# The first element of a two-stage graph kernel: another order of its loads, biases as rows, and the residual added on VectorE

## The chip, the cores and the metric

The kernel runs on one NeuronCore of a Trainium2 chip. It has five engines with an instruction stream each: TensorE (PE, matmuls; PEld in a profile is its weight load), VectorE (DVE), ScalarE (ACT), GpSimd (POOL) and SyncE (SP). SP issues most of the DMA transfers; GpSimd and ScalarE can issue some too. The metric is device time of one execution, in microseconds (us); lower is better. The kernel before took 2397.51 us, the median of three runs from 2396.07 to 2399.57 us.

## The reference, cut to what matters

Sixteen independent elements b, each with node features x (1024 x 128) and a dense matrix adj (1024 x 1024), all float32. Two stages, each with a residual and a layer norm without scale:

```
# stage 0
degree = adj.sum(-1)
nb     = einsum('id,ij->jd', x, adj) / degree
x1     = layernorm(x + relu(concat(x, nb) @ W.T + b))
# stage 1: four layers; layer l sees x1 or earlier layers' outputs
src = f @ ws + bs ;  dst = f @ wd + bd ;  own = f @ wn + bn
src_agg = (adj / row_norm) @ src          # rows scaled to length 1
dst_agg = (adj / column_norm).T @ dst     # columns scaled to length 1
f_next  = tanh(concat(src_agg, own, dst_agg) @ wu + bu)
# result
out = layernorm(x1 + f_4)
```

Stage 0 needs adj and x of the element, W (128 x 256) and b. Stage 1 needs for every layer the products of its weights with wu ("folded" weights), made once in the first element, and row and column norms of adj.

## The kernel before, in words

The order of work on every engine is written out by hand (manual_schedule, line 1041). Elements are run one after another; while element b is in its four layers, the loads, row sums, squares and stage 0 of element b + 1 are placed between its matmuls through "hooks". The first element has nothing ahead of it to hide in, so its stage 0 and the weight folding stand in a prologue of their own, lines 1047 to 1239, and parts of them in the hooks of its first layer (lines 1251 to 1306). The change touches only these.

**The loads of the prologue.** adj of element 0 is 4 MB. It is cut in two halves h of 512 rows, each half in two "row pairs" (PAIRS, in the order h = 1 and then h = 0), and every pair in G = 4 groups g of 32 partitions: a pair is four transfers of 256 KB (load_pair, lines 1054 to 1057). x is cut in the same way into eight transfers of 64 KB (load_nodes). Groups 0 and 1 (partitions 0 to 63) go on SP's queue, groups 2 and 3 (partitions 64 to 127) on GpSimd's. SP's order is: w0n (W, 128 KB), two groups of x for each half, two groups of each of the four pairs, b0c (the bias b), and then for each layer its weights and biases (fetch_weights, line 180), between them adj once more in another layout (load_rows, four times 1 MB). A bias is 128 values that go to one value on each partition, so one transfer of 128 pieces of 4 bytes; there are 17 of them. SP issues through eight completion semaphores in turn: a transfer is issued only when the one eight places ahead of it has landed.

**Its matmuls.** PE first transposes W (w0tr, lines 1102 to 1105), then for each half transposes x (to_xT), starts the residual's bank with x times the identity (with_x, line 1165) and starts pw, W's first half times x (weights_of_x, line 1157). Then the "gathers" (line 1131), 16 matmuls of 128 x 512 that sum x over the rows of adj, four for each row pair. ScalarE squares the rows of each pair, VectorE sums them (squares_of). The inverse degrees are spread over partitions by transposes (degree_row, factor_bank at line 354); scaled, weights_of_agT and with_y (line 1171, which adds the transposed result to the residual's bank) end stage 0 of a half; norm_stats and norm_write or norm_write_act make x1n, to_x1 its transpose.

**The weights.** fold_begin (line 199) and fold_end (line 222) make a layer's folded weights: transposes and small products on PE, copies by ScalarE, both through the two banks of small(). Layers 0 and 1 are folded in the prologue, 2 and 3 in hooks 5, 8, 9 and 12 of the first layer (lines 1302 to 1304). messages (line 686) makes the layer's messages in four groups; plain_layer (line 827) is the first element's first layer, whose products are d (destination, on a) and z (source, on at). row_factors0 (line 1252) gathers the inverse row norms, rinv, with which scale_rows scales the second copy of adj on ScalarE; transpose_rows turns it into at on VectorE.

## Time and profile before

One execution was profiled: 2396.57 us, of which 2394.8 us are the span from the first to the last instruction; 1.77 us lie around it.

| | before |
|---|---|
| median of three runs | 2397.51 us |
| the profiled execution, and its span | 2396.57 us, 2394.8 us |
| busy: PE, DVE, ACT, POOL | 2377.7, 2089.2, 980.3, 273.8 us |
| PE's first gather begins at | 13.31 us |
| PE busy from 13.3 to 20.0, 20 to 30, 30 to 40 us | 6.69, 9.97, 9.67 us |
| PE busy from 40 to 50, 50 to 60, 60 to 70 us | 8.40, 9.76, 9.80 us |
| PE and DVE busy from 100 to 120 us | 17.79, 18.14 us |

Times in the views are counted from the start of the span. A row of a timeline gives the start, the duration, the engine, the line of code, the operation with what it writes and reads, and how many instructions were joined; in brackets stands the idle time before it and what ended it. A matmul of float32 appears as two records. "SPq" rows are SP issuing a transfer, not the transfer itself.

### The profile page before, as it was taken

What the parts mean: (1) busy time and instruction counts of PE and PEld (TensorE: products, weight loads), DVE (VectorE), ACT (ScalarE), POOL (GpSimd) and SP (SyncE); (2) the same over time, 40 slices, a digit from 0 to 9 for tenths busy, and PEclk for the clock granted to TensorE, in tenths of its full rate; (3) what the DMA queues carried; (4) which work ended last, traced back from release to release, by engine and by line L of the source; (5) the groups of instructions that cost most, each with busy time, mean ns of one, the idle gap of its engine ahead of it and who ended that gap; (6) DMA issues with size and microseconds to landing.
All of it is one profiled execution on the core that took longest, in us unless ns stands there. A gap on an engine that the chain in (4) does not pass through costs nothing.

```text
span 2394.8 us, 39324 instructions
## 1 busy us (share of the span) xinstructions
PE 2377.7 (99%) x15293; PEld 1288.4 (54%) x15293; DVE 2089.2 (87%) x2814; ACT 980.3 (41%) x1842; POOL 273.8 (11%) x102
## 2 busy tenths in 40 slices
PE   8999999999999999999999999999999999999998
PEld 4444554645556455554655546455464555645555
DVE  5998888999889989889988889888899888998954
ACT  5524345253343524435244452534525344352322
POOL 4101111001111011110111110111100111101110
PEclk9999999999999999999999999999999999999999
DMA  9527244262633627335272442634426253362400
GB/s 206 123 75 146 69 114 90 70 148 57 137 75 81 138 48 157 61 97 116 55 163 56 107 97 71 147 69 111 91 69 151 57 132 78 80 141 48 100 22 22
DMA packets 365897, 232.03 MB, mean 97 GB/s; under 512 B 152784, under 2 KB 336848, under 8 KB 365712
## 3 DMA queue, kind: packets, MB, share of 16 engines
q1 hardware_dynamic: 364944, 227.16, 42.6%
q0 software_dynamic: 768, 2.36, 0.4%
q8 instruction: 121, 1.98, 0.4%
q14 instruction: 64, 0.52, 0.1%
HBM read 209.59 MB, written 19.84 MB: 96 GB/s over the span
## 4 chain that ended last, share of the span: by engine, by line
PE 95%; DVE 2%; DMA 1%; SPq 1%; issue 1%; ACT 0%; POOLq 0%; DVEq 0%
PE m L1005 40%; PE z L1005 29%; PE pt L247 9%; PE pt_z L247 5%; PE m_f L583 5%; PE z_f L583 2%; PE pw L247 2%; PE m3s L1005 1%; PE z L851 1%; DMA wm<-in_L_gnn_ws_dram 1%; PE pt_p L247 1%; SPq L640 1%; DVE acc L331 0%; DMA a<-in_adj_dram 0%; PE d L851 0%
## 5 line engine op out<-in xcount | busy, mean ns | idle before, releaser
L1005 PE MATMUL m<-a,t 128*64 128x512 f32 x1008 | 434.6, 593 | 0.2 <-DVE t L711 0.2
L1005 PE MATMUL m<-at,t 128*64 128x512 f32 x1008 | 418.5, 592 | 0.0
L1005 PE MATMUL m<-Q,S 128*64 128x512 f32 x880 | 394.0, 593 | 0.0
L1005 PE MATMUL m<-T,S 128*64 128x512 f32 (+1 forms) x1040 | 393.5, 573 | 0.0
L456 POOL TENSOR_TENSOR rs<-ve,mhalf 128x32 f32<-128x32 f32 x30 | 191.9, 6396 | 987.9 <-DVE ve L454 987.9
L1005 PE MATMUL z<-at,t 128*64 128x512 f32 x504 | 229.2, 592 | 0.0
L1005 PE MATMUL z<-at,S 128*64 128x512 f32 x504 | 228.3, 593 | 0.0
L1005 PE MATMUL z<-a,S 128*64 128x512 f32 x504 | 228.2, 593 | 0.0
L1005 PE MATMUL z<-a,t 128*64 128x512 f32 x504 | 227.2, 593 | 0.0
L1005 PE MATMUL z<-Q,t 128*64 128x512 f32 x504 | 227.0, 593 | 0.0
L1005 PEld LDWEIGHTS m<-T,S 128*64 128x64 f32 x1040 | 131.0, 137 | 128.5 <-issue 126.5
L1005 PEld LDWEIGHTS m<-Q,S 128*64 128x64 f32 x880 | 118.2, 137 | 147.9 <-issue 141.0
L1005 PEld LDWEIGHTS m<-a,t 128*64 128x64 f32 x1008 | 131.9, 137 | 108.7 <-issue 100.0
L1005 PEld LDWEIGHTS m<-at,t 128*64 128x64 f32 x1008 | 131.3, 137 | 109.4 <-issue 108.0
L1005 PE MATMUL z<-T,t 128*64 128x512 f32 x384 | 172.8, 592 | 0.0
L884 ACT COPY e<-m 64x512 f32<-64x512 f32 x63 | 36.6, 582 | 327.9 <-PE m L1005 327.5
L376 POOL TENSOR_TENSOR inv<-cols,mhalf 128x16 f32<-128x16 f32 (+1 forms) x17 | 46.8, 2752 | 1031.2 <-DVE cols L375 1031.2
L414 DVE TENSOR_TENSOR a<-a,cinv 128x512 f32<-128x512 f32 x250 | 154.1, 694 | 1.9 <-ACT cinv L351 1.3
L322 ACT ACTIVATE sq<-a 128x1024 f32<-128x1024 f32 x120 | 125.9, 1050 | 37.1 <-DVE acc L329 23.2
L247 PE MATMUL pt<-wm,f1T 128*64 128x128 f32 (+1 forms) x1536 | 133.8, 309 | 0.0
L247 PEld LDWEIGHTS pt<-wm,f1T 128*64 128x64 f32 x1536 | 110.3, 137 | 31.9 <-issue 12.3
L317 ACT ACTIVATE a<-a 128x1024 f32<-128x1024 f32 x120 | 125.3, 1045 | 0.4
(302 smaller groups left out, 5019.8 us busy)
## 6 DMA issues: line engine op xcount, KB each, us to landing
a<-in_adj_dram SPq DMA_DIRECT2D x120, 512.0 KB, 12.3
rows<-in_adj_dram SPq DMA_DIRECT2D x480, 64.0 KB, 2.1
a<-in_adj_dram SPq DMA_DIRECT2D x240, 128.0 KB, 3.5
wm<-wsave SPq DMA_DIRECT2D x32, 704.0 KB, 5.0
wm<-wsave SPq DMA_DIRECT2D x31, 320.0 KB, 3.2
xn<-in_x_dram SPq DMA_DIRECT2D x124, 64.0 KB, 5.5
xs<-in_x_dram SPq DMA_DIRECT2D x60, 128.0 KB, 3.6
cinv<-dr SPq DMA_DIRECT2D x30, 256.0 KB, 6.4
```

The costliest lines, as they stand in the source:

```text
L247: nc.tensor.matmul(out[s], x[:, s], y, start=start, stop=stop)
L317: nc.scalar.activation(a[:, i, :], a[:, i, :], AF.Copy, accum_out=degree)
L322: nc.scalar.activation(sq, a[:, i, :], AF.Square, accum_out=state["cols"][:, i:i + 1])
L376: nc.gpsimd.tensor_tensor(inv[:, s], cols[:, s], mhalf[:, s], ALU.pow)
L414: engine.tensor_mul(a[:, i, s], a[:, i, s], cinv[:, s])
L456: nc.gpsimd.tensor_tensor(rstd, ve, mhalf[:, :n], ALU.pow)
L583: nc.tensor.matmul(o, x_, y_, start=start, stop=stop)
L640: nc.sync.dma_start(piece[g * C:(g + 1) * C, :, h * P:(h + 1) * P], v[h, g, :, k:k + n])
L851: nc.tensor.matmul(nodes(o) if len(y.shape) == 4 else o, x_, y, start=start, stop=stop)
L884: nc.scalar.copy(e0[high], A[high])
L1005: nc.tensor.matmul(o, x, y_, start=start, stop=stop)
```

## The change: another order of loads, and work moved within the first element

- x goes first: the half h = 1 on SP's queue, h = 0 on ScalarE's queue; none on GpSimd's.
- All four groups of the first row pair go on SP's queue. Of the other three pairs groups 0 and 1 stay on SP's, 2 and 3 on GpSimd's. w0n is issued after the second pair's two groups.
- Biases are loaded as rows of 128 values (load_biases): nine on GpSimd's queue ahead of its row pairs, eight on SP's between the weights of layers 1 and 2. One PE transpose for each set (bias_columns) and a ScalarE copy turn them into columns. The 17 transfers of 4-byte pieces are gone. The weights of layer 1 come before the first second copy of adj.
- PE begins with two matmuls on zeros (idle). The transposes of W come after both to_xT, and stay ahead of weights_of_x and of the gathers.
- The residual is no longer summed in PSUM: with_x transposes yT and VectorE adds xn into x1n (a 128 x 512 addition for each half); the norm then reads x1n and writes it in place. The two matmuls of x by the identity are gone.
- square(second) moves behind weights_of_agT(0). fold_begin and fold_end of layer 2 and rinv's gathering move from the first layer's hooks 5 and 8 and from row_factors0 into the gaps of messages; layer 2's weight sums move from hook 11 to hook 6.

The core of the diff:

```diff
--- before.py
+++ after.py
@@ -177,7 +177,7 @@
 
         return wm if l in PAIRED else wm[:, :KEPT[l] * 2 * P].rearrange("p (c v) -> p c v", v=2 * P)
 
-    def fetch_weights(raw, l, q, wm=None):
+    def fetch_weights(raw, l, q, bc, wm=None):
         ws, bs, wd, bd, wn, bn, wu, bu = layers[l]
         nch = CHUNKS[l]
         size = max(3 * nch * P, KEPT[l] * 2 * P, WIDTH[l])
@@ -187,9 +187,6 @@
             q.dma_start(wr[:, k], w.rearrange("(c p) v -> p c v", p=P))
         wur = raw.take(3 * P).rearrange("p (k v) -> p k v", k=3)
         q.dma_start(wur, wu.rearrange("(c p) v -> p c v", p=P))
-        bc = raw.take(4)
-        for k, v in enumerate((bs, bd, bn, bu)):
-            q.dma_start(bc[:, k:k + 1], v.rearrange("(p o) -> p o", o=1))
         if wm is not None:
             wm = as_chunks(wm, l)
         else:
@@ -1051,33 +1048,55 @@
     xv = [x[0, half(h)].rearrange("(g k c) d -> g c k d", g=G, c=C) for h in range(NH)]
     PAIRS = [(h, k) for h in (1, 0) for k in range(0, BPH, 2)]
 
-    def load_pair(q, pair, groups):
-        h, k = pair
+    def load_pair(q, i, groups):
+        h, k = PAIRS[i]
         for g in groups:
             q.dma_start(a[g * C:(g + 1) * C, h * BPH + k:h * BPH + k + 2], av[h][g, :, k:k + 2])
 
-    def load_nodes(q, h, groups):
-        for g in groups:
+    def load_nodes(q, h):
+        for g in range(G):
             q.dma_start(xn[g * C:(g + 1) * C, h * BPH:(h + 1) * BPH], xv[h][g])
 
+    idle = one.tile([P, HW], F32, tag="S2", name="idle")
+    nc.vector.memset(idle, 0.0)
+    make_identity(nc, ident)
+    load_nodes(nc.sync, 1)
+    load_nodes(nc.scalar, 0)
+    load_pair(nc.sync, 0, range(G))
+    load_pair(nc.sync, 1, (0, 1))
     nc.sync.dma_start(w0n, w0)
-    shares = ((nc.sync, range(G // 2)), (nc.gpsimd, range(G // 2, G)))
-    for h in (1, 0):
-        for q, groups in shares:
-            load_nodes(q, h, groups)
-    make_identity(nc, ident)
-    for pair in PAIRS:
-        for q, groups in shares:
-            load_pair(q, pair, groups)
-    nc.sync.dma_start(b0c, b0.rearrange("(p o) -> p o", o=1))
+    load_pair(nc.sync, 2, (0, 1))
+    load_pair(nc.sync, 3, (0, 1))
+    biases_of = [[b0, *layers[0][1::2], *layers[1][1::2]], [*layers[2][1::2], *layers[3][1::2]]]
+    in_rows = one.tile([P, HW], F32, tag="S3", name="biases")
     raw = Raw()
+    columns = [raw.take(len(v)) for v in biases_of]
+    bcs = [columns[0][:, 1:5], columns[0][:, 5:], columns[1][:, :4], columns[1][:, 4:]]
+
+    def load_biases(i, q):
+        for k, v in enumerate(biases_of[i]):
+            q.dma_start(in_rows[k:k + 1, i * P:(i + 1) * P], v.rearrange("(o p) -> o p", o=1))
+
+    def bias_columns(i):
+        n = len(biases_of[i])
+        pt = small(f"biases{i}")
+        nc.tensor.transpose(pt[:, :n], in_rows[:n, i * P:(i + 1) * P], ident[:n, :n])
+        nc.scalar.copy(columns[i], pt[:, :n])
+        if i == 0:
+            nc.scalar.copy(b0c, pt[:, :1])
+
+    load_biases(0, nc.gpsimd)
+    for i in (1, 2, 3):
+        load_pair(nc.gpsimd, i, (2, 3))
     wm = message_tile("wm1_0")
     Q = combined(0, "Q")
     places = {q: Q[i].rearrange("p k (u c) -> p (k u) c", u=2) for q, i in ((2, 2), (3, 3), (0, 4))}
     places[1] = one.tile([P, 2 * NJ, HW // 2], F32, tag="T2", name="rows1_0")
     rows, fetched = {}, []
-    for l, q in enumerate((None, 2, 3, None)):
-        fetched.append(fetch_weights(raw, l, nc.sync, None if l else wm))
+    for l, q in enumerate((None, None, 2, 3)):
+        if l == 2:
+            load_biases(1, nc.sync)
+        fetched.append(fetch_weights(raw, l, nc.sync, bcs[l], None if l else wm))
         if q is not None:
             rows[q] = load_rows(0, q, [places[q]])
     wm = as_chunks(wm, 0)
@@ -1099,10 +1118,15 @@
             nc.tensor.transpose(pt[:, q * P:(q + 1) * P], xn[:, h * BPH + q], ident)
         nc.scalar.copy(nodes(xT[:, half(h)]), blocks(pt))
 
-    pt = small("w0tr", [HW])
-    for k in range(2):
-        nc.tensor.transpose(pt[:, k * P:(k + 1) * P], w0n[:, k * P:(k + 1) * P], ident)
-    nc.scalar.copy(w0T.rearrange("p k v -> p (k v)"), pt[:, :2 * P])
+    pt = product("idle")
+    for _ in range(2):
+        nc.tensor.matmul(pt, idle[:, :P], idle, start=True, stop=True)
+
+    def transposes_of_w0():
+        pt = small("w0tr", [HW])
+        for k in range(2):
+            nc.tensor.transpose(pt[:, k * P:(k + 1) * P], w0n[:, k * P:(k + 1) * P], ident)
+        nc.scalar.copy(w0T.rearrange("p k v -> p (k v)"), pt[:, :2 * P])
 
     sq = []
     for p in (3, 4):
@@ -1164,14 +1188,12 @@
 
     def with_x(h):
 
-        pn[h] = ps_t.tile([P, BPH, P], F32, tag="pt", name=f"yn0_{h}")
-        nc.tensor.matmul(pn[h].rearrange("p q d -> p (q d)"), ident, xn[:, h * BPH:(h + 1) * BPH].rearrange("p q d -> p (q d)"),
-                         start=True, stop=False)
-
-    def with_y(h):
+        pt = ps_t.tile([P, BPH, P], F32, tag="pt", name=f"yn0_{h}")
         for q in range(BPH):
             i = h * BPH + q
-            nc.tensor.matmul(pn[h][:, q], yT[:, i * P:(i + 1) * P], ident, start=False, stop=q == BPH - 1)
+            nc.tensor.transpose(pt[:, q], yT[:, i * P:(i + 1) * P], ident)
+        pn[h] = x1n[:, h * BPH:(h + 1) * BPH]
+        nc.vector.tensor_add(pn[h], pt, xn[:, h * BPH:(h + 1) * BPH])
 
     def to_x1(h):
         pt = product(f"x1tr_{h}")
@@ -1179,19 +1201,22 @@
             nc.tensor.transpose(pt[:, q * P:(q + 1) * P], x1n[:, h * BPH + q], ident)
         nc.scalar.copy(x1T[:, half(h)], pt)
 
-    for h in (1, 0):
-        to_xT(h)
-        with_x(h)
-        weights_of_x(h)
-    for pair in PAIRS[:2]:
-        squares_of(*pair)
-        gathers_of(*pair)
+    to_xT(1)
+    to_xT(0)
+    transposes_of_w0()
+    weights_of_x(1)
+    weights_of_x(0)
+    squares_of(*PAIRS[0])
+    gathers_of(*PAIRS[0])
+    squares_of(*PAIRS[1])
+    gathers_of(*PAIRS[1])
     nc.vector.tensor_add(sq[6], sq[6], sq[7])
     add_square(5)
     add_square(6)
     degree_inverses(1)
     degree_row(1)
     squares_of(*PAIRS[2])
+    bias_columns(0)
     gathers_of(*PAIRS[2])
     add_square(0)
     add_square(1)
@@ -1206,27 +1231,27 @@
     gather(0, first)
     weights_of_agT(1)
     square(first)
-    square(second)
     gather(0, second)
     add_square(first)
-    with_y(1)
     scaled(0)
+    with_x(1)
     weights_of_agT(0)
     stats = {1: norm_stats(pn[1], range(BPH), "0_0_1", True)}
+    square(second)
     fold_begin(0, fetched[0])
-    with_y(0)
+    with_x(0)
     fold_end(0, fetched[0])
     stats[0] = norm_stats(pn[0], range(BPH), "0_0_0")
     root_inverses(cols, inv, slice(NB))
     add_square(second)
     biases = fold_begin(1, fetched[1], nc.vector.tensor_copy, True)
     for q in range(BPH):
-        norm_write_act(x1n[:, BPH + q], pn[1][:, q], stats[1], q)
+        norm_write_act(pn[1][:, q], pn[1][:, q], stats[1], q)
     to_x1(1)
     biases()
     fold_end(1, fetched[1])
     for q in range(BPH):
-        norm_write(x1n[:, q], pn[0][:, q], stats[0], q)
+        norm_write(pn[0][:, q], pn[0][:, q], stats[0], q)
 
 
     kept = scratch.tile([N, D], F32, tag="kept", name="kept0")
@@ -1250,13 +1275,23 @@
         f1 = feature(b, "f1T")
         if b == 0:
             def row_factors0():
-                nonlocal rinv
-                rinv = gather_inverses(0, row_inverses(0, inv))
                 column_sums(0, st0)
                 for q in (2, 3):
                     scale_rows(rows[q], q, rinv)
 
-            t = messages(b, 0, feats, wm, {0: lambda: to_x1(0), 2: row_factors0}, with_sums=False)
+            def second_x1():
+                to_x1(0)
+                bias_columns(1)
+                fold_begin(2, fetched[2])
+                ahead["spread"] = row_inverses(0, inv)
+
+            def factors_and_fold():
+                nonlocal rinv
+                fold_end(2, fetched[2])
+                rinv = gather_inverses(0, ahead["spread"])
+
+            ahead = {}
+            t = messages(b, 0, feats, wm, {0: second_x1, 1: factors_and_fold, 2: row_factors0}, with_sums=False)
             cinv = {}
 
             def columns0(rows, h, engine=nc.vector):
@@ -1265,15 +1300,15 @@
             def rows0(destination, finish):
                 for q in (2, 3):
                     transpose_rows(rows[q], q, at)
-
-            def cinv0(destination, finish):
-                cinv[0] = factor_rows_now(0, 1, inv, "cinv")
-
-            def second0(destination, finish):
-                columns0(range(NJ, NB), 1)
                 sums_of_weights(2, fetched[2][3])
                 weight_sums(own_seven(2, fetched[2][3]))
                 nc.sync.dma_start(wsave[2], fetched[2][3])
+
+            def cinv0(destination, finish):
+                cinv[0] = factor_rows_now(0, 1, inv, "cinv")
+
+            def second0(destination, finish):
+                columns0(range(NJ, NB), 1)
                 destination(1, cinv[0])
                 columns0(range(NJ), 1)
 
@@ -1299,8 +1334,8 @@
             def folded(l, part):
                 return lambda *_: part(l, fetched[l])
 
-            hooks = {4: lambda *_: inverses(0, st0, NB), 5: folded(2, fold_begin), 6: rows0, 7: cinv0,
-                     8: folded(2, fold_end), 9: lambda *_: fold_and_scale(3, 0), 11: second0, 12: folded(3, fold_end),
+            hooks = {4: lambda *_: inverses(0, st0, NB), 6: rows0, 7: cinv0,
+                     9: lambda *_: fold_and_scale(3, 0), 11: second0, 12: folded(3, fold_end),
                      14: lambda *_: scale_rows(rows[1], 1, rinv), 18: first0, 26: sums0}
             T = combined(0, "T")
             plain_layer(b, 0, feats, t, wm, a, at, f1, "acc", hooks)
```

More of the change, by code (lines that the diff above doesn't have):

```diff
@@ L1267, in rows0 @@
                     transpose_rows(rows[q], q, at)
+                sums_of_weights(2, fetched[2][3])
+                weight_sums(own_seven(2, fetched[2][3]))
+                nc.sync.dma_start(wsave[2], fetched[2][3])
             def cinv0(destination, finish):
@@ L1273, in second0 @@
                 columns0(range(NJ, NB), 1)
-                sums_of_weights(2, fetched[2][3])
-                weight_sums(own_seven(2, fetched[2][3]))
-                nc.sync.dma_start(wsave[2], fetched[2][3])
                 destination(1, cinv[0])
```

## The prediction

> **What bounds the kernel now.** I read the busy shares, then the engines' timelines of the first 120 us, then SP's timeline and the DMA bytes in short windows. The page:
>
> ```profile
> PE 2377.7 (99%) x15293; PEld 1288.4 (54%) x15293; DVE 2089.2 (87%) x2814; ACT 980.3 (41%) x1842; POOL 273.8 (11%) x102
> ```
>
> PE is the bound of the whole and the other fifteen elements are untouched, so only what moves PE's work of the first element counts. The opening of PE's timeline, and its start of the first layer:
>
> ```profile
> 5.98 1.91 PE L1168 MATMUL yn<-xn,ident 128*128 128x512 f32 x2
> ...
> 10.24 1.03 PE L1168 MATMUL yn<-xn,ident 128*128 128x512 f32 x2
> 11.11 1.10 PE L1159 MATMUL pw<-x_T,w0T 128*128 128x512 f32 x2
> 13.31 7.11 PE L1132 MATMUL pa<-a,xn 128*128 128x512 f32 x16 [1.10 <-issue]
> 20.45 0.62 PE L359 MATMUL dinv<-ident,inv 128*128 128x128 f32 x4
> ...
> 41.31 0.31 PE L252 MATMUL rp<-sp,fold 128*64 128x32 f32 x4 [0.89 <-DVE sp L381]
> ```
>
> The gathers start at 13.31, when the first row pair has landed (VectorE's first sum starts at 13.30, after 8.19 us of waiting for adj). From there PE has work almost without a gap: 8 gathers in 7.11 us are 0.85 us each plus 0.28 lost. So the start of the gathers, S, sets the end, and later only small stalls are to be had (0.89 before rp, 0.70 behind ScalarE at layer 2's fold). Early matmuls are slow: the 128x512 of 5.98 takes 1.70 until the next begins, that of 10.24 takes 0.87.
>
> SP's timeline gives the landings, since each issue waits for the transfer eight places ahead:
>
> ```profile
> 8.19 0.35 SPq L1072 DMA_DIRECT2D b0c<-in_L_gnn_b_dram  x1
> 9.29 0.35 SPq L187 DMA_DIRECT2D wm<-in_L_gnn_ws_dram  x1
> 10.23 0.33 SPq L187 DMA_DIRECT2D wm<-in_L_gnn_wd_dram  x1
> 12.23 0.33 SPq L187 DMA_DIRECT2D wm<-in_L_gnn_wn_dram  x1
> ...
> 19.64 0.33 SPq L192 DMA_DIRECT2D raw<-in_L_gnn_bn_dram  x1
> ...
> 22.97 0.33 SPq L187 DMA_DIRECT2D raw<-in_L_gnn_ws_dram  x1
> ```
>
> SP's groups of pairs 0 and 1 land at 8.19, 9.29, 10.23 and 12.23, its last group at 19.64; ws of layer 0, issued at 9.29 and only 64 KB, lands at 22.97, behind all that was issued before it. The queue keeps its order. The DMA view of 10 to 15 us, with both queues at work, and of 72 to 74 us, where SP alone loads adj of the next element in the same 32-partition groups:
>
> ```profile
> DMA packets 451, 1.51 MB, mean 302 GB/s; under 512 B 82, under 2 KB 82, under 8 KB 451
> ...
> DMA packets 119, 0.42 MB, mean 211 GB/s; under 512 B 16, under 2 KB 16, under 8 KB 119
> ```
>
> From 70 to 86 us it is 199 to 221, some 206 GB/s. In 10 to 15 us SP's queue moved 0.76 MB of the 1.51, so 152 GB/s.
>
> [...]
>
> **The change, part by part.** I write times against S where they follow from it.
>
> *x and the idle matmuls.* x's 0.52 MB starts at about 1.8 as before and is in by about 4.6. idle occupies PE from 1.3 to 4.7 (two at 1.70), the eight x transposes end near 6.5 (four took 0.9 at 5.10). Before, that front ended at 12.2 and waited for adj, so what it saves is worth nothing by itself.
>
> *The first pair on SP.* 1.05 MB from about 4.3 at 206 GB/s is 5.1 us: moved by 9.4. Landings lag the bytes: SP had moved 1.44 MB (its bytes up to pair 1's second group) at about 10.2 and landed them at 12.23, and the other groups lag 1.7 to 2.5. So it lands near 11, against 13.3: 2.3 us to be had, no more.
>
> *W behind the second pair.* w0tr stays ahead of pw and of the gathers in PE's order, and w0n is now eleventh on SP's queue: 0.26 (x) + 1.05 + 0.52 + 0.13 = 1.97 MB, with ScalarE's 0.26 beside it 2.23 MB. Until GpSimd's transfers flow I count 0.62 MB by 5.0 (0.69 were moved before) and 206 GB/s. GpSimd starts after ident at about 1.9, issues nine bias transfers at 0.53 to 0.60 (a transfer of adj costs it 0.527, four of x 2.39) until 6.8; its first adj bytes came 1.2 (x) to 3.4 us (adj, issued 4.25, flowing from 7.7) after issue, so 8 to 10.2, taken 9.5: 1.55 MB by then. The remaining 0.68 MB at 152 GB/s is 4.4 us: 13.9. With a lag of 1.7 w0n lands at 15.6. Bounds: 13.3 (GpSimd later, no lag) and 17.2 (GpSimd at 7.5, lag 2.5).
>
> *From W to the gathers.* PE is idle from 6.5 to 15.6, so I take half clock: transposes to ScalarE's copy 0.73 (4.34 to 5.07), copy 0.37, handover 0.1, two pw at 1.70: 4.6 us, and 0.1 for gathers still at half clock. S = 15.6 + 4.7 = 20.3, against 13.31: +7.0. With a warm clock it is 0.45 + 0.47 + 1.71 = 2.6 and S is 18.2. Behind w0tr stand also ScalarE's w0T copy and, behind that, its squares of pair 0, from W + 1.2: four take 4.4 us, over by S + 0.9, before dinv at S + 6.8. Pair 1 is in by 14.7, wanted at S + 3.4; the last pair by 23, wanted near S + 11. The loads no longer stall the gathers: the 0.28 us goes. The transposes of the bias rows add about 0.15 to PE (nine and eight columns; two dinv transposes of 128 columns take 0.23). Sum so far +6.9.
>
> *The residual.* Two 128x512 matmuls by the identity went in the front, worth nothing. VectorE gains two additions at 0.69 (agT, same shape). Half 1: yT's transposes end at S + 16.4, addition to 17.2, statistics (1.6) 18.8, ve 19.1, GpSimd's power 1.04 and product 0.2 to S + 20.4; ScalarE comes to x1n only after layer 0's copies at S + 21.1 (34.29 before is S + 21.0). Half 0: norm_write at S + 23.0, before S + 22.9. Cost nothing, covered by ScalarE's fold copies; without that cover 0.7. square(second) behind yT(0) lets yT(0) come 0.5 earlier and layer 0's copies 0.7 later; wm0 stands at S + 19.7 either way.
>
> *Layer 2's fold into messages.* It leaves the d products: 47.28 to 49.49 and 53.02 to 54.36, 3.55 us with its 0.70 stall. In messages it adds 2.8 us of PE and stalls behind ScalarE's copies and two small banks of about 0.9, and takes up the old 0.89 before rp and 0.9 more: x1tr's end to the first z was 4.0, and becomes 5.9 (bias and first transposes to S + 25.5, second after the bias copy 26.45, biases 27.25, pt 28.1, wm 29.0, rp 29.35, two pt 31.05). Gain 3.55 − 1.9 = 1.65. VectorE gets rinv 0.9 later and its weight sums earlier, and stands at S + 45 with the destination product either way; at 74.70 it waited 1.72 us for PE, so it follows. Bounds: 0 (VectorE doesn't follow) and 2.5.
>
> *4-byte transfers gone.* SP's queue is shorter by 9 issues and the rows come some 8 us earlier; they had 5 us in hand before (Q's third quarter landed by 52.5, used at 57.95). Nothing; uncovered they could cost S's own delay at most.
>
> Sum: +7.0 − 0.28 + 0.15 − 1.65 = +5.2 us, on its own execution 2396.57 → 2401.8; on the median 2397.51, 0.94 above it, 2402.7. I say 2402.5.
>
> **Rivals.** (1) *PE stays warm, or W lands at its early bound*: +3.1 or +2.9, so about 2400.5. For it: the clock's fall back isn't shown here. Against: 9 us idle is long beside the 5.7 us of slow start. (2) *W isn't held behind adj* (the other side): if w0n lands no later than the first pair, at 11, the gathers start there and wait 0.3 us for pair 1 (moved by 13.0, landed at 14.7, wanted 3.4 after the start): 11.3 − 13.31 − 0.13 − 1.65 = −3.8, so 2393.7; were there no lag, pair 1 at 13.0 would set 9.6 and −5.5. It decides from w0n at 10.4 downwards, where the sum above is zero. Against it: ws kept its place in the queue. (3) *GpSimd's half comes too late*: nine small transfers cost more than counted, and pair 1's groups 2 and 3 land after S + 3.4 = 23.7, from when each us is lost; and the fold's gain isn't realised: +7 to +10, 2406. Against: 9 us in hand. (4) *The 1.65 us aren't kept* alone: 2404. It lies within the main case.
>
> **How the numbers follow.** Main case 0.74, own range 2400 to 2405.5; rival 1 0.09; rival 2 0.07; rival 3 0.10. About 0.2% (4.8 us) is what a measurement can tell from no change, so the bound lies at 2402.3, inside the main case: 0.45 of its 0.74 over it, 0.29 within. Slower 0.45 + 0.10 = 0.55; within 0.29 + 0.09 + 0.04 = 0.42; faster 0.03 of rival 2. The range 2398.5 to 2407 takes in rival 1 and most of rival 3 and leaves out rival 2 and the tails.
>
> **What would show it.** In the changed profile: two idle matmuls, x transposes near 5 to 6.5, then a long PE gap that ends with w0n's transfer and not with adj; w0tr near 15.6, pw at 1.70 each, first pa near 20, while VectorE's first sum of a row starts near 11; no gap between the gathers; x1n, d and z at their old distance from S, less 1.65 from the first d on; from 130 us on the same distances. It is wrong if the gathers start with VectorE's first sum, if pw takes 0.86, or if PE waits inside the gathers for GpSimd's groups.

## The result, and the profile after

The changed kernel takes 2402.44 us (median of ten executions, 2401.21 to 2405.02) against 2396.52 us for the kernel before in the same comparison: a ratio of 1.0024, 95% interval 1.0014 to 1.0034, which holds the 0.2% that the prediction took as the bound. The profiled execution took 2402.13 us with a span of 2400.3 us, 5.5 us more than before's 2394.8.

The busy shares of the page for the changed kernel show how much of this counts as work:

```profile
PE 2380.4 (99%) x15287; PEld 1292.3 (54%) x15287; DVE 2091.5 (87%) x2817; ACT 980.6 (41%) x1845; POOL 276.1 (12%) x105
```

PE is busy 2.7 us longer with six records fewer: matmuls at a slower pace count as busy too (in the timeline below the four records of pw at 15.43 take 3.78 us, the four of z at 52.23, of the same size, 1.98). The other 2.8 us are idle, and PE's timeline of the changed kernel shows where (start, duration, engine, line, what it writes and reads, records joined, and in brackets the idle time ahead with what ended it):

```profile
1.46 3.78 PE L1123 MATMUL idle<-idle 128*128 128x512 f32 x4 [1.46 <-DVE mhalf L1106]
5.53 1.72 PE L1118 MATMUL xtr<-ident,xn 128*128 128x128 f32 x8 [0.29 <-DMA xn<-in_x_dram]
14.31 0.66 PE L1128 MATMUL w0tr<-ident,w0n 128*128 128x128 f32 x2 [7.06 <-DMA w0n<-in_L_gnn_W_dram]
15.43 3.78 PE L1183 MATMUL pw<-x_T,w0T 128*128 128x512 f32 x4 [0.46 <-ACT w0T L1129]
19.00 7.79 PE L1156 MATMUL pa<-a,xn 128*128 128x512 f32 x16
26.63 0.60 PE L356 MATMUL dinv<-ident,inv 128*128 128x128 f32 x4
27.16 0.23 PE L1083 MATMUL biases<-ident,biases 9*128 9x9 f32 x1
...
39.91 0.94 PE L224 MATMUL wm<-raw 128*128 128x128 f32 x6 [0.75 <-ACT raw L203]
...
45.04 0.66 PE L1201 MATMUL x1tr<-ident,x1n 128*128 128x128 f32 x4
...
52.23 1.98 PE L848 MATMUL z<-x_T,wm 128*128 128x512 f32 x4
...
68.63 5.32 PE L848 MATMUL d<-a,t 128*128 128x512 f32 x12
```

After x's transposes PE stands for 7.06 us, and W's transfer ends that. From there to the gathers are 4.69 us (w0tr, ScalarE's copy of w0T, two pw at 1.78 each). The gathers begin at 19.00; before they began at 13.31. From the first of them to dinv it is 7.63 us, before 7.14 (20.45 less 13.31). VectorE, in its own timeline, had the first row pair much earlier:

```profile
10.58 2.35 DVE L1149 TENSOR_REDUCE cols<-a 128x1 f32<-128x1024 f32 x2 [8.46 <-DMA a<-in_adj_dram]
17.24 2.35 DVE L1149 TENSOR_REDUCE cols<-a 128x1 f32<-128x1024 f32 x2 [4.32 <-DMA a<-in_adj_dram]
```

So the first pair did come 2.7 us earlier than before (10.58 against 13.30), and PE did not use it: its instruction order has W ahead of the gathers, and W came at 14.3. The second pair came only at 17.24. The windows of the changed kernel (PE, PEld, DVE, ACT, POOL busy with counts, then PEclk, DMA share, GB/s) show the pause:

```profile
10.00:15.00 5.00, 0.66 (x2) 0.29 (x2) 2.35 (x2) 0.00 (x0) 0.91 (x3) 0.53 1.06 234
15.00:20.00 5.00, 4.57 (x6) 1.99 (x7) 2.76 (x3) 4.54 (x9) 2.37 (x1) 0.50 1.04 297
```

From 10 to 15 us PE has 0.66 us of work. The DMA engines are full (share 1.06), but at 234 GB/s where before had 302. SP's queue had them nearly alone up to 11 us, as the changed kernel's transfers between 8 and 9 us show, by queue (q1 is SP's, q0 GpSimd's; packets, MB, share of the time of the 16 engines):

```profile
q1 hardware_dynamic: 63, 0.20, 100.1%
q0 software_dynamic: 36, 0.00, 4.0%
```

GpSimd had issued its first group of adj at 6.04, but up to 11 us its queue moves only small packets of the bias rows (0.00 MB). From 11 to 12 us it moves 0.03 MB, from 12 to 13 us 0.14 MB; the rate of before, some 300 GB/s, is reached from 14 us on (307 GB/s from 14 to 15).

Now the distances, before against after. Start of the gathers: +5.69. Half 0's transposes of x1 (x1tr): 37.89 against 45.04, +7.15. First z: 42.45 against 52.23, +9.78. Start of the last unbroken run of d products, behind layer 3's fold: 62.48 against 68.63, +6.15; VectorE's transposes of acc near 112 us: +6.14, then +5.99 near 250 us and +5.89 near 2154 us. The lines of the kernel before:

```profile
37.89 0.66 PE L1179 MATMUL x1tr<-ident,x1n 128*128 128x128 f32 x4
...
42.45 1.98 PE L851 MATMUL z<-x_T,wm 128*128 128x512 f32 x4
...
62.48 5.32 PE L851 MATMUL d<-a,t 128*128 128x512 f32 x12
```

### The profile page after: what moved, and what is told of

It reads as the page before. It is cut to its first block, busy times and chain, and to the rows that moved or that the text cites. A ratio compares the mean times of both kernels' runs of the same rounds, so it can differ in the third digit from the quotient of the medians.

```text
span 2400.3 us, 39331 instructions
## 1 busy us (share of the span) xinstructions
PE 2380.4 (99%) x15287; PEld 1292.3 (54%) x15287; DVE 2091.5 (87%) x2817; ACT 980.6 (41%) x1845; POOL 276.1 (12%) x105
## 3 DMA queue, kind: packets, MB, share of 16 engines
q8 instruction: 121, 1.98, 0.4%
## 4 chain that ended last, share of the span: by engine, by line
PE 95%; DVE 2%; DMA 1%; ACT 1%; issue 0%; SPq 0%; POOLq 0%; ACTq 0%; DVEq 0%
PE m L1002 40%; PE z L1002 28%; PE pt L244 9%; PE pt_z L244 5%; PE m_f L580 5%; PE z_f L580 2%; PE pw L244 2%; DMA a<-in_adj_dram 1%; PE z L848 1%; PE m3s L1002 1%; PE pt_p L244 1%; PE d L848 0%; DMA Q<-in_adj_dram 0%; DVE acc L328 0%; ACT a L314 0%
```

## The experiments

Except where noted, an edit is to the changed kernel. Each group was measured beside the kernel before, whose median was 2395.85 us (the first four below), 2396.35 (the fold alone, the residual alone and both with two queues), 2396.09 (the residual with its matmuls put back, and the pairs in halves) and 2396.45 us (W first with the square back, and the last one). A ratio compares with that kernel.

### W first on SP's queue

```diff
+    nc.sync.dma_start(w0n, w0)
     load_nodes(nc.sync, 1)
...
     load_pair(nc.sync, 1, (0, 1))
-    nc.sync.dma_start(w0n, w0)
```

> The changed kernel with w0n issued first on SP's queue, nothing else. Theory (w0n behind 1.8 MB of the same queue holds the transposes of W, and these hold the gathers on PE): w0n is in by about 3, the gathers start with the first pair, which lands 0.6 us later than in the changed kernel (10.6 + 0.6 = 11.2), then wait about 2.7 us for the second pair, whose half on GpSimd's queue lands at 17.2 as before; that is worth a start at 13.9 without a wait, 6 us less than the changed kernel's 19.0 + 1.0: 2396.5 us. Rival (the gate is not W but something else that stands ahead of the gathers, the half clock or ScalarE): the gathers stay near 19 and the time near 2402.4.

Measured: 2395.66 us, ratio 1.0000 (0.9991 to 1.0008). PE's timeline of this kernel:

```profile
6.68 1.94 PE L1118 MATMUL xtr<-ident,xn 128*128 128x128 f32 x8 [1.45 <-DMA xn<-in_x_dram]
8.45 0.69 PE L1128 MATMUL w0tr<-ident,w0n 128*128 128x128 f32 x2
9.60 3.64 PE L1183 MATMUL pw<-x_T,w0T 128*128 128x512 f32 x4 [0.46 <-ACT w0T L1129]
13.08 7.03 PE L1156 MATMUL pa<-a,xn 128*128 128x512 f32 x16
```

Moving one transfer of 128 KB gives 5.9 us back of a start that was 5.69 late. So W's place in the queue is the cause: PE let nothing pass ahead of W's transposes (it stood for 7.06 us in the changed kernel, with the first pair in at 10.58). It doesn't make a gain: the first pair is there at 12.39, but PE is still at pw, at half pace (3.64 us for its four records).

### The first pair's gathers ahead of W

```diff
-    transposes_of_w0()
-    weights_of_x(1)
-    weights_of_x(0)
     squares_of(*PAIRS[0])
     gathers_of(*PAIRS[0])
+    transposes_of_w0()
+    weights_of_x(1)
+    weights_of_x(0)
```

> The changed kernel with the transposes of W and both weights_of_x moved behind the first pair's gathers, on PE and on ScalarE; the loads are as in the changed kernel. Theory (PE's order makes w0n's landing at 14.3 cost): the first gather starts at about 10.6 at half clock, four of them end at 16 to 16.6, W and the two products follow until 19, the second pair's gathers start there: worth a start at 15.7, 2398.1 us, between 2396.5 and 2399.5. Rival (the loads themselves set the start): no gain, 2402.

Measured: 2398.34 us, ratio 1.0009 (1.0002 to 1.0016). With the loads as in the changed kernel and only PE's order turned round, PE begins with the first pair:

```profile
10.72 6.17 PE L1156 MATMUL pa<-a,xn 128*128 128x512 f32 x8 [4.25 <-DMA a<-in_adj_dram]
16.73 0.38 PE L1128 MATMUL w0tr<-ident,w0n 128*128 128x128 f32 x2
17.57 1.98 PE L1183 MATMUL pw<-x_T,w0T 128*128 128x512 f32 x4 [0.46 <-ACT w0T L1129]
```

So the wait was one of order and not of data. Four gathers (x8) take 6.17 us, where the second pair's take 3.60 later in the same kernel: behind the idle time of 4.25 us it is the gathers that go at half pace here, and pw behind them is quick (1.98 for four records).

### W first, and the bias rows last on GpSimd's queue

The edit of the first experiment, and:

```diff
-    load_biases(0, nc.gpsimd)
     for i in (1, 2, 3):
         load_pair(nc.gpsimd, i, (2, 3))
+    load_biases(0, nc.gpsimd)
```

> As the run with w0n first, and the nine bias transfers issued behind GpSimd's row pairs. Theory ([...] adj flows there only from 11 us on although it is issued at 6): adj flows on GpSimd's queue from 3 to 5 us, both queues together at 270 to 300 GB/s, the first pair lands at 11 to 12, the second at 13.6 to 15, no wait inside the gathers: 2394.5 us, 2 below the run with w0n first. Rival (GpSimd's adj is late because SP's backlog comes first, whatever stands ahead of it): 2396.5, and the second pair at 17.

Measured: 2401.82 us, ratio 1.0025 (1.0015 to 1.0035). This was a miss by 7 us, in the wrong direction. PE's timeline:

```profile
11.92 1.94 PE L1118 MATMUL xtr<-ident,xn 128*128 128x128 f32 x8 [6.68 <-DMA xn<-in_x_dram]
```

x, the first thing needed, lands 5 us later than with the rows ahead (11.92 against 6.68). The transfers of this kernel between 7 and 8 us, by queue:

```profile
q0 software_dynamic: 66, 0.21, 106.3%
q1 hardware_dynamic: 7, 0.00, 2.5%
```

GpSimd's adj did flow from 3 us on, as expected, and took the DMA engines: SP's queue, with the rest of x in pieces of 512 bytes, gets 2.5%. adj goes in pieces of 4 KB. (It was not so from the start: from 5 to 6 us SP's and ScalarE's queues, both with x in pieces of 512 bytes, had 26.2% and 33.2% beside GpSimd's 56.8%.) With the nine small transfers ahead of adj in GpSimd's queue (W first) that queue had still only 2.2% from 7 to 8 us, with x in by 6.68: they had been keeping x's way free.

### Six more matmuls between x's and W's transposes

```diff
     to_xT(0)
+    for _ in range(6):
+        nc.tensor.matmul(idle_bank, idle[:, :P], idle, start=True, stop=True)
     transposes_of_w0()
```

> The changed kernel with six more matmuls on zeros between the transposes of x and those of W, so that PE is busy until about 13.5. Theory (9 us of idle PE brought the clock back to half): the two products of x take 0.87 each in place of 1.78, the gathers start at 16.9 in place of 19.0 and run at 0.85, 3 us saved: 2399.4 us. Rival (the clock's part is small): 2402.

Measured: median 2401.18 us (2398.06 to 2403.54), ratio 1.0022 (1.0013 to 1.0030). The profiled execution took 2399.01 us, and there the effect is as expected:

```profile
14.33 0.41 PE L1128 MATMUL w0tr<-ident,w0n 128*128 128x128 f32 x2 [2.18 <-DMA w0n<-in_L_gnn_W_dram]
15.21 1.98 PE L1183 MATMUL pw<-x_T,w0T 128*128 128x512 f32 x4 [0.46 <-ACT w0T L1129]
17.03 7.03 PE L1156 MATMUL pa<-a,xn 128*128 128x512 f32 x16
```

W lands where it did (14.3), the gap ahead of it is 2.18 us in place of 7.06, pw goes at full pace, gathers start 1.97 us earlier and dinv comes 6.86 us after them in place of 7.63. This execution is 3.1 us below the changed kernel's profiled one, the median only 1.3 below its median. A possible reading is that in some executions the pace fell behind that gap, and in others, as in this one, it did not. The granted clock of the twelve executions agrees: its mean is 1.000 in the three fastest (2398.06 to 2399.01 us) and 0.997 to 0.999 in the nine others (2400.24 us and more). No profile of a slower execution was taken, so where the pace fell in those stays open.

### The kernel before, with layer 2's fold moved alone

```diff
-            t = messages(b, 0, feats, wm, {0: lambda: to_x1(0), 2: row_factors0}, with_sums=False)
+            t = messages(b, 0, feats, wm, {0: second_x1, 1: factors_and_fold, 2: row_factors0}, with_sums=False)
...
-            hooks = {4: lambda *_: inverses(0, st0, NB), 5: folded(2, fold_begin), 6: rows0, 7: cinv0,
-                     8: folded(2, fold_end), 9: lambda *_: fold_and_scale(3, 0), 11: second0, 12: folded(3, fold_end),
+            hooks = {4: lambda *_: inverses(0, st0, NB), 6: rows0, 7: cinv0,
+                     9: lambda *_: fold_and_scale(3, 0), 11: second0, 12: folded(3, fold_end),
```

The functions named are those of the changed kernel, without the bias transposes; the weight sums move as there.

> The kernel before with only layer 2's fold moved into the first messages. As worked out ahead of the result: -1.65 us (2394.2 on 2395.85 of the runs before). By the profile after, where the stretch from x1tr to the first z grew by 2.63 us and the d products lost 3.63: -1.0 us (2394.9). Rival: VectorE doesn't follow and the gain is 0 (2395.9). Told by the stretches: first z late by 1.9 or by 2.6 us, VectorE's place at the end of the d products early by 1.65, 1.0 or 0.

Measured: 2394.80 us against 2396.35, ratio 0.9996 (0.9988 to 1.0004). The comparison of medians can't tell this from no change; the distances in the trace can. PE's timeline, where the fold now stands and where it stood:

```profile
39.56 0.71 PE L209 MATMUL bm<-raw 128*128 128x128 f32 x4 [0.40 <-ACT raw L206]
...
42.89 0.31 PE L252 MATMUL rp<-sp,fold 128*64 128x32 f32 x4
43.03 1.93 PE L247 MATMUL pt<-wm,x_T 128*64 128x256 f32 x16
44.89 1.98 PE L851 MATMUL z<-x_T,wm 128*128 128x512 f32 x4
...
48.76 2.84 PE L851 MATMUL d<-a,t 128*128 128x512 f32 x6
...
61.30 5.32 PE L851 MATMUL d<-a,t 128*128 128x512 f32 x12
```

rp no longer waits its 0.89 us, but ScalarE's copy costs 0.40 in its place, and first z is 2.44 us later (44.89 against 42.45). The last run of d products begins at 61.30 against 62.48, so from the first z to there 3.62 us are saved (16.41 in place of 20.03). The gain is 1.18 us there and in VectorE's transposes near 112 us, and some 1.65 us from 250 us to the last such transpose. The step of 0.5 between them stands near 130 us. VectorE of the kernel before waits there, by the profile for a transfer of x:

```profile
130.81 9.72 DVE L414 TENSOR_TENSOR a<-a,cinv 128x512 f32<-128x512 f32 x16 [0.55 <-DMA xn<-in_x_dram]
```

and in this execution of the fold alone the same instructions begin without a wait:

```profile
129.10 9.72 DVE L414 TENSOR_TENSOR a<-a,cinv 128x512 f32<-128x512 f32 x16
```

That the moved fold removes this wait is not shown: the changed kernel has the fold moved too and waits 0.41 us there, W first 0.26.

### The kernel before, with the residual on VectorE alone

```diff
     for h in (1, 0):
         to_xT(h)
-        with_x(h)
         weights_of_x(h)
...
-    with_y(1)
     scaled(0)
+    with_x(1)
```

The rest is as in the changed kernel's with_x and norm writes.

> The kernel before with only the addition of x moved from TensorE to VectorE (four transposes into PSUM and one addition for each half, the two matmuls by the identity gone from the front). As worked out ahead of the result: 0 us (2395.9), the gathers at 13.3 as before because they wait for adj, and x1tr at its old 37.9 because ScalarE's fold copies cover the addition. Rival: the addition of 0.7 us is on the path, x1tr 0.7 later, 2396.6.

Measured: 2399.06 us, ratio 1.0010 (1.0002 to 1.0019), so 2.7 us slower. Neither expectation holds. VectorE's addition isn't where the time goes: from the dinv transposes to x1tr of half 0 the trace has 17.36 us, before 17.44. It goes ahead of that: pair 0 is in 0.67 us later in this execution (gathers from 13.98), and from the first gather to dinv it is 9.43 us in place of 7.14. The gathers' records of this kernel, by the tile they write, from 15 to 17 us:

```profile
L1132 PE MATMUL pa<-a,xn x4: 1061/1061/1190, 14.0 to 16.7; 128*128 128x512 f32 x4
```

and the kernel before, in the same stretch:

```profile
L1132 PE MATMUL pa<-a,xn x6: 592/593/597, 14.7 to 16.8; 128*128 128x512 f32 x6
```

(min, median and max of one in ns). A record of the same matmul takes 1061 ns in place of 593. The two matmuls of x by the identity were not only the residual's first half: they were work that had TensorE at full pace when the first row pair came. Without them it had not reached that pace at all: each pw takes 2.07 us for its two records, at 6.57 and at 10.50, where before's second took 1.10. PEclk of this kernel says 1.00 throughout, as it also does over the changed kernel's first matmuls on zeros, whose records take 1061 ns and more (0 to 5 us). So ahead of the first rise the pace is read here from the matmuls themselves.

### The same, with those two matmuls put back into a bank that nothing reads

```diff
         to_xT(h)
+        pt = product(f"idle{h}")
+        nc.tensor.matmul(pt, ident, xn[:, h * BPH:(h + 1) * BPH].rearrange("p q d -> p (q d)"), start=True, stop=True)
         weights_of_x(h)
```

> The run with the residual alone, with the two 128x512 matmuls by the identity put back where they stood in the front, into a bank that nothing reads. Theory: the addition on VectorE costs 0 and the 2.6 us of that run are TensorE's clock, which without those two matmuls fell to half before the gathers; with them back pw takes 0.87 each, eight gathers 7.1 again, x1tr at 37.9 and the time is 2396.4, that of the kernel before. Rival: the cost is the addition on VectorE or the transposes; then it stays at 2398.9.

Measured: 2397.11 us, ratio 1.0003 (0.9995 to 1.0012): 1.7 of the 2.7 us come back against the runs before of each group. PE's timeline:

```profile
7.38 1.18 PE L1159 MATMUL pw<-x_T,w0T 128*128 128x512 f32 x2
...
9.69 1.10 PE L1159 MATMUL pw<-x_T,w0T 128*128 128x512 f32 x2
13.62 8.80 PE L1132 MATMUL pa<-a,xn 128*128 128x512 f32 x16 [2.82 <-issue]
```

pw runs at full pace as expected, earlier than before even; then PE is idle for 2.82 us ahead of the gathers, where before had 1.10, and dinv comes 8.64 us after the first gather, in place of 7.14. From 13 to 15 us they take 662 to 668 ns, then 1057 ns until about 17 us, then 592. So TensorE fell back after the pause, and late: about 1 us after the gathers had begun. PEclk, in windows of 1 us, agrees: 1.00 up to 14 us, then 0.76, 0.50, 0.50, 0.54, and 1.00 again from 18 us on. From dinv to x1tr it is 17.35 us again. The addition is free, as the rival denied; of the 1.7 us that are left in the trace 1.5 are the pace and 0.3 a later pair 0. The profiled execution, 2398.25 us, is the slowest of the thirteen, and five took 2396.25 to 2396.45, so the pace may not have fallen in every one.

### W, x and the first pair on two queues

```diff
+    nc.scalar.dma_start(w0n, w0)
     load_nodes(nc.sync, 1)
     load_nodes(nc.scalar, 0)
-    load_pair(nc.sync, 0, range(G))
+    load_pair(nc.scalar, 0, (2, 3))
+    load_pair(nc.sync, 0, (0, 1))
     load_pair(nc.sync, 1, (0, 1))
-    nc.sync.dma_start(w0n, w0)
...
-    load_biases(0, nc.gpsimd)
+    load_biases(0, nc.gpsimd, range(4))
+    load_pair(nc.gpsimd, 1, (2, 3))
+    load_biases(0, nc.gpsimd, range(4, 9))
```

and one idle matmul more ahead of x's transposes and one behind W's.

> The changed kernel with W first on ScalarE's queue, the first pair in both partition halves at once (groups 0 and 1 on SP's queue, 2 and 3 on ScalarE's), the second pair's groups 2 and 3 after four of GpSimd's bias rows, and one idle matmul more before x's transposes and one between W's transposes and pw. x, W and pair 0 are 1.70 MB; at 302 GB/s that is 5.6 us from 1.8, with a lag of 1.7 some 9.2 for pair 0. If adj on two queues sets the start, gathers start at 10 to 11, against 13.08 with W first alone, and the time is 2393.3 (2392.5 to 2394.5). Rivals: ScalarE's issues hold its copies of xT, and the start stays at 13 (2395.7); or GpSimd's 4 KB pieces starve the 512 B pieces of x as in the run with the biases last, start 15 or later (2398 or more).

Measured: 2398.68 us, ratio 1.0008 (1.0002 to 1.0015). A miss. PE's timeline:

```profile
6.45 0.60 PE L1123 MATMUL xtr<-ident,xn 128*128 128x128 f32 x4
11.45 1.12 PE L1123 MATMUL xtr<-ident,xn 128*128 128x128 f32 x4 [4.40 <-DMA xn<-in_x_dram]
```

Half 1 of x, on SP's queue, is in by 6.45, half 0, on ScalarE's behind W, at 11.45. Between 6 and 7 us SP's queue has 76.8% of the DMA time and ScalarE's 12.2%. That looks like the run with the bias rows last, where adj's 4 KB pieces on another queue held up x's 512-byte ones, but it isn't shown here: from 7 to 8 us ScalarE's queue already moves adj itself (34 packets, 0.09 MB), so most of x was through by then, and only its last pieces, behind adj on three queues, land as late as 11.45.

### The same, with the last row's square back ahead of yT

```diff
     square(first)
+    square(second)
     gather(0, second)
...
     stats = {1: norm_stats(pn[1], range(BPH), "0_0_1", True)}
-    square(second)
```

> The same with the square of the last adj row back ahead of the first half's last layer step on ScalarE, as in the kernel before. If the 0.75 us stall of TensorE before layer 0's third folded product comes from this square standing behind yT, the stall goes and the time is 0.5 us below that of the run without it (2392.8); otherwise the stall stays and the times are equal.

Measured: 2398.11 us, ratio 1.0007 (0.9999 to 1.0016). From the start of the gathers to x1tr of half 0 it is 24.64 us, without the edit 25.27: the 0.75 us wait ahead of wm, layer 0's folded product, is gone from the trace and 0.63 us with it.

### W first, with the square back

The edit of the first experiment, and:

```diff
     stats = {1: norm_stats(pn[1], range(BPH), "0_0_1", True)}
-    square(second)
```

with the square where the kernel before has it, as above.

> The run with W first, with the square of the last adj row back ahead of the last layer step of half 0 on ScalarE. Theory: that square behind yT is what TensorE waits 0.75 us for ahead of layer 0's third folded product; put back, the time from the start of the gathers to x1tr of half 0 falls by 0.6 as it did with the two queues (25.3 to 24.7), and the time is 0.6 below that of the run with W first (2395.7 to 2395.1). Rival: the 0.75 reappears as a wait for statistics or x1n, and the time stays at 2395.7.

Measured: 2395.59 us against 2396.45, ratio 0.9995 (0.9986 to 1.0003). The same distance is 24.65 us, in the run with W first 25.31. PE's timeline of this kernel has no wait ahead of the product any more:

```profile
13.26 7.03 PE L1156 MATMUL pa<-a,xn 128*128 128x512 f32 x16
...
32.50 0.83 PE L224 MATMUL wm<-raw 128*128 128x128 f32 x6
```

Up to x1tr, moving the square behind yT costs 0.66 us: ScalarE does it just when the copies for layer 0's fold are wanted. The whole time shows it less well. The gathers began 0.18 us later in this execution; its lead over W first is 0.45 us near 112 us, 0.25 near 250 us and nothing at the last of VectorE's transposes, and both spans are 2393.8 us. The medians stand 0.86 and 0.19 us under those of the kernel before beside them, with intervals that overlap.

### The pairs in halves on SP's and GpSimd's queues

W first on SP's, x as in the changed kernel, the square back, and:

```diff
-    load_pair(nc.sync, 0, range(G))
+    load_pair(nc.sync, 0, (0, 1))
...
-    load_biases(0, nc.gpsimd)
-    for i in (1, 2, 3):
+    load_biases(0, nc.gpsimd, range(4))
+    for i in (0, 1):
+        load_pair(nc.gpsimd, i, (2, 3))
+    load_biases(0, nc.gpsimd, range(4, 9))
+    for i in (2, 3):
         load_pair(nc.gpsimd, i, (2, 3))
```

> The changed kernel with W first on SP's queue, the first two pairs' groups 2 and 3 on GpSimd's queue behind four bias rows (five more rows behind them), groups 0 and 1 on SP's, one idle matmul more in the front and one between W's transposes and pw, and the square of the last adj row back ahead of the last layer step of half 0. x should land near 6.7 as with W first, since four small transfers hold GpSimd's 4 KB pieces back until then; pair 0 at 10 to 11 over both halves; pw at full clock; gathers from 11 against 13.08; 0.6 from the square: 2393.0 (2392.3 to 2394.0). Rival: GpSimd's pieces come into x's time and x lands at 10 or later as in the run with ScalarE's queue: gathers from 15, 2397. Second rival: the clock is half again by the gathers for want of work between x's transposes and W's, then 2394.5.

Measured: 2396.13 us, ratio 1.0000 (0.9992 to 1.0008). Pair 0 is in at 11.42, but x's transposes only begin at 8.23, and with W, the added matmul and pw behind them gathers start at 13.65. They then wait 1.09 us for the third pair. The pace fell here too, after an idle time of 2.05 us, and was back before the gathers; the added matmul takes 1061 ns for a record:

```profile
8.23 1.51 PE L1123 MATMUL xtr<-ident,xn 128*128 128x128 f32 x8 [2.05 <-issue]
...
10.04 1.92 PE L1212 MATMUL idle<-idle 128*128 128x512 f32 x2
```

### The same, with the pairs ahead of the rows and half of pw behind the first pair

```diff
     weights_of_x(1)
-    weights_of_x(0)
     squares_of(*PAIRS[0])
     gathers_of(*PAIRS[0])
+    weights_of_x(0)
```

GpSimd's third pair ahead of its last five rows, no added matmul ahead of pw, and the rows' transposes behind the third pair's gathers.

> The run with the pairs in halves on SP's and GpSimd's queues, without the idle matmul ahead of pw, with pw of half 0 behind the first pair's gathers, the first three pairs ahead of GpSimd's last five bias rows, and those rows' transposes behind the third pair's gathers. Gathers start at 11.4 to 11.8 when pair 0 is in, less 0.9 for the later pw, so 1.3 us ahead of that run, and the 1.09 us that TensorE waited for pair 2 go: 2396.1 - 2.4 = 2393.7 (2392.8 to 2394.8). Rivals: pair 3 is late behind the five rows and the 1.1 come back there (2394.8); TensorE's clock has fallen by the first gathers (2395.5).

Measured: 2396.38 us, ratio 1.0000 (0.9992 to 1.0009). The gathers start where they should, at full pace, and it gains nothing:

```profile
11.28 3.67 PE L1160 MATMUL pa<-a,xn 128*128 128x512 f32 x8 [1.17 <-DMA a<-in_adj_dram]
14.79 1.02 PE L1187 MATMUL pw<-x_T,w0T 128*128 128x512 f32 x2
15.64 3.60 PE L1160 MATMUL pa<-a,xn 128*128 128x512 f32 x8
21.10 0.62 PE L356 MATMUL dinv<-ident,inv 128*128 128x128 f32 x4 [1.86 <-DVE inv L1157]
...
25.91 1.98 PE L1160 MATMUL pa<-a,xn 128*128 128x512 f32 x4 [0.60 <-DMA a<-in_adj_dram]
```

What is won at the start is lost behind it in this kernel: 1.86 for the inverse degrees, which VectorE makes after an addition of two squares (3.10 us here, 1.22 in the kernel above with W first and the square back), and 0.60 for the last pair. With the gathers at 11.28, VectorE's chain and the arrival of adj were what TensorE waited for. No version tried is faster than the kernel before by more than the comparison can tell; the lowest medians against it are those of the fold alone (0.9996) and of W first with the square back (0.9995).

## Why the prediction was right

It forecast 2402.5 us; the median is 2402.44, and its own execution 2402.13 against the 2401.8 of its sum. The mechanism holds: W behind two pairs, PE's order behind W. The first two experiments show it from both sides. But that the sum is so close is in part luck. Its terms miss by more, in opposite directions; and as a change it was +5.0 us against the measured +5.9, since the kernel before came out 1.0 us lower in the comparison (2396.52 against 2397.51).

- **W's landing**, 15.6 predicted, 14.3 measured, inside the bounds of 13.3 and 17.2: 1.3 too late. SP's queue had the DMA engines alone longer than assumed: GpSimd's adj was taken to flow from 9.5 and flowed from about 11.5. The nine rows ahead of it cost more than their issue, which was over by 6.04. With 11.5 in the same sum W lands at 15.0 (an estimate). Of the other 0.7, some 0.3 are bytes moved sooner still (W's pieces had moved by about 13) and 0.4 a shorter lag from there to the landing.
- **From W to the gathers**, 4.7 predicted, 4.69 measured, at half clock as assumed (pw's two at 1.78 each). That PE falls to it behind an idle time was the author's estimate; the profile before shows no fall. Behind the gap of 7.06 us the trace of the changed kernel does: PEclk falls at about 10.3 us (0.64 from 10 to 11, then 0.50) and is back at about 20.5 (0.74 from 20 to 21). But gaps of 2.82 us (the residual with its matmuls put back, PEclk down to 0.50 from 15 to 17 us) and of 2.05 us (the pairs in halves) were enough for a fall, where 2.13 us (the fold alone) and 2.18 us (six more matmuls) were not. So the length of a gap alone doesn't decide; what else does, and why the fall came late in one of them, these runs don't show.
- **The gathers themselves** were forecast 0.28 shorter than before, with 0.1 for half pace in the step ahead. To dinv they took 0.49 longer: 7.63 us, where before had 7.14 with its stall and W first has 6.88 without half pace or stall. So the stall on loads did go, and half pace cost 0.75 where 0.1 was counted; taken together, the two had the wrong sign. Pair 1 was in only at 17.24 where 14.7 was forecast; wanted at about 23, that was hidden. The late-half rival (3) thus had its cause right, and more than 5 us of cover left.
- **The bias transposes**: 0.15 predicted, 0.16 measured (27.16 to 27.32). From one dinv to the next, though, it is 5.94 us in place of 5.61, in this and in the runs that kept the bias transposes there and had no wait on loads, so they may have cost up to 0.33; no run takes them out alone.
- **The residual costs nothing**: the cover it named is right, 17.35 and 17.36 us against 17.44 for the same distance. But the step before it said that the two matmuls by the identity "went in the front, worth nothing". In the kernel before that is wrong: taken out alone they cost 2.3 us of pace. In the changed kernel W's wait buries the point.
- **square(second)**: the prediction said that wm0 stands where it did either way. Up to x1tr it cost 0.66 us, shown by putting the square back. Layer 0's copies come later because of it, and wm0 with them. So the distance from the first gather to x1tr grew by 1.46 us: 0.49 (pace less stall), 0.16 (biases), 0.66 (square) and some 0.15 that no run separates, all of it between the two dinv.
- **Layer 2's fold**: 3.55 saved and 1.9 added were predicted, for 1.65. At the last run of d products 3.63 were saved and 2.63 added (2.44 alone), so 1.0; alone 1.18. The step that failed is what messages take up: with the fold alone it adds 1.97 and 1.56 us there (38.34 to 40.31 and 41.33 to 42.89), near the 3.7 counted, and the old 0.89 ahead of rp goes as said, but of the "0.9 more" only some 0.2 is found. The term is 0.5 to 0.65 short there. Alone, it is 1.65 from 250 us on, but that this meets the forecast is chance: the last 0.5 is the wait of 0.55 us near 130 us that is missing there. In the changed kernel that wait is 0.41, so 0.15 of the step is seen.
- **The rival of the other side**, W not held, was priced at 2393.7 us. W first gives 2395.66: x's landing at 6.7 and pw at half pace put the start at 13.1 and not at 11.3. Where it did start at 11.3, later waits took it back. Even without its fault the change had about nothing to win, as far as these runs go.

At 112 us the terms add up: 5.2 predicted, less 1.3 (W), plus 0.77 (the gathers, 0.49 against -0.28), 0.66 (the square), 0.15 (not separated) and 0.65 (the fold) make 6.1; measured 6.14. The difference of the two spans is 5.5: 0.15 came back near 130 us, 0.1 by 2154 us, and another 0.4 only behind the last of VectorE's transposes; these last two are not explained here.

## What to carry to other kernels

When loads are reordered, follow the engine's instruction order too: the first instruction whose data were late decided here, whatever was already there behind it (7.06 us for W, with the first pair in at 10.58). Ask of each matmul in a front whether it is also what keeps TensorE at pace (without two of them a record of the gathers took 1061 ns in place of 593), and read the pace from the duration of a like matmul. Before a queue of large pieces is let loose earlier, look at which small-piece transfer is in flight on the other queue (x came in at 11.92 in place of 6.68).

## What the runs showed of the hardware that was not expected

- Queues didn't always share alike. With 4 KB pieces on both, before's queues had 52.1% and 51.6% from 10 to 15 us. With W first and the bias rows last, pieces of 512 bytes on two queues had 59.4% beside 56.8% for one queue of 4 KB pieces from 5 to 6 us; from 7 to 8 us SP's had 2.5% beside 106.3%, 7 packets beside 66, with the last of its x still to come. On how many of the engines SP's queue had work then, and what changed at 6 us, no view shows.
- With nine transfers of 512 bytes ahead of it in GpSimd's queue, adj's first bytes came some 5 us after it was issued (6.04 to about 11.5). The small packets passed slowly beside 4 KB pieces: 24 to 36 in 1 us from 7 to 10 us, where W first, with 512-byte pieces on the other queues, had 106 from 4 to 5 us. With four ahead, at that earlier time, adj issued at 3.62 moves 0.16 MB from 5 to 6 us (the pairs in halves). With none the first bytes come within 2 us (issued from 1.53, flowing at 3).
- A matmul of 128 x 512 took 593 ns (before, from 15 to 17 us) or 1061 ns (the residual alone, there) for each of its two records. An idle gap of 2.82 us ahead of it, and in another kernel one of 2.05 us, was followed by the second; gaps of 1.10, 1.17, 2.13 and 2.18 us in other profiles, with TensorE at full pace ahead of them, were not.
